# An empty piece between turning a tile and turning it back, in the last batch's first eight heads

## The chip, the cores and the metric

The kernel runs on one core of a Trainium2 chip. The metric is the device time of one execution in microseconds; the median of four runs stands for the kernel.

## The reference, cut to what matters

Two layers work on eight batches of 512 tokens of width 256. The first has a state-space mixer and a mixture of experts; the second has attention and another mixture of experts. The change lies in the second layer's attention, at its end:

```
scores = clip(q_h . k_h / 16) * decay(|i - j|)       # 16 heads of width 16, 512 x 512
attn   = softmax(scores)
out_h  = attn . v_h                                  # 512 x 16 for each head
y      = concat_heads(out_h) @ Wo                    # 256 x 256
x      = x + y + mixture_of_experts(xn)
```

Neither layer's other parts differ between the two kernels.

## The kernel before

The second layer is one hand-written order of instructions for all engines, made by Python generators while the kernel is built. The main loop runs over n = 0 to 130. The 128 steps are 8 batches x 4 groups of four heads x 4 tiles of 128 query rows; three more rounds of the loop drain what is left. The last batch (b = 7) has the steps 112 to 127.

In round n the loop issues, in this order:

1. The scores of step n: TensorE multiplies q and k for four heads (`s_ps`, line 1471), VectorE clamps each (line 1476), multiplies it by the decay band while taking its row maximum (line 1478), and negates the maxima (`ng`, line 1482). That is one block of nine instructions on VectorE, and ScalarE's exponentials of this step wait for its end.
2. The exponentials of step n - 1 on ScalarE (line 1486): heads 0 and 1, later 2, later 3.
3. In even rounds the values product of the two steps before (`o_ps`, line 1502).
4. The transposes of step n - 2, head by head: four 128x128 products into one of two banks (`p_ps`, line 1493), which ScalarE copies out (`pT`, line 1494). Heads 0 and 1 come first, then 2, then 3.

Between these stand slots, each a call of `fill()`. A call takes the first generator in a list of waiting work and runs it to its next `yield`; what is issued until then is one piece. The list `urgent` goes ahead of all else. An odd round has three slots: behind the scores, behind the transposes of heads 0 and 1, and at the end. An even round has four: behind the values, behind heads 0 and 1, between heads 2 and 3, and at the end. A generator that is at its end gives its slot to the next one. In the rounds up to 117 the slots hold the pieces of the experts; in 119 and 120 they hold the output projection of batch 6 (`finish`, line 1434).

For the batches 0 to 6 the division by the softmax's sum goes through memory (`divide`, line 1508). The last batch is divided on the chip. The values product of a group leaves 128 rows (four heads of 32 rows, of which 16 are output and one is the sum of the softmax) by 512 tokens, copied to `ol` (line 1515). When the second group is copied, in round 122, `first_heads` (line 1386) is put ahead in `urgent`. For each of the four tiles of 128 tokens it turns the two groups (`tq`, line 1392), so that tokens lie on the partitions; `columns` divides on VectorE (`smq`, line 1381, and `oq`, line 1383); and a second piece turns the result back (`tb`, line 1396), which ScalarE copies to `oT` (line 1397), the input of the output projection. `tq` and `tb` share one bank of PSUM (`bank`, one buffer), so that each waits for the reader of the one before. Here they are called tq0, tb0, ..., tq3, tb3.

Every engine works its instructions in the order in which they were issued. The class `Ending` (line 1400) does the same for the last eight heads, in the tail behind round 128, and `project` (line 1423) writes the last batch's output.

Of the kernel before, what the change touches and what calls it, by code (L numbers as in the profile page):

```python
# [59 lines left out]
def tile_kernel(ctx: ExitStack, tc: tile.TileContext, t, out: bass.AP):  # L60
# [292 lines left out]
    def bank(name, shape, tag="gen"):  # L353
        return mp.tile(shape, FP, name=name, tag=("e", "s")[tag] if isinstance(tag, int) else tag, bufs=2)
# [807 lines left out]
    with tc.tile_pool(name="a1", bufs=1) as p1, tc.tile_pool(name="a2", bufs=2) as p2, tc.tile_pool(  # L1162
# [214 lines left out]
        def columns(tq):  # L1377

            tq = tq.rearrange("p g (i r) -> p (g i) r", r=32)
            sm = p2.tile([P, 8], FP, name="smq", tag="smq")  # L1380
            V.reciprocal(sm, tq[:, :, AD])
            oq = p2.tile([P, 8, AD], FP, name="oq", tag="oq")
            V.tensor_tensor(oq, tq[:, :, :AD], bc(sm, 2, [P, 8, AD]), ALU.mult)
            return oq.rearrange("p h d -> p (h d)")

        def first_heads(oT, os):

            for c in range(TPB):
                at = slice(c * P, (c + 1) * P)
                tq = bank("tq", [P, 2, P])  # L1390
                for k in range(2):
                    T.transpose(tq[:, k, :], os[k][:, at], ident)
                oq = columns(tq)
                yield
                tp = bank("tb", [P, P])
                T.transpose(tp, oq, ident)
                A.copy(oT[:, 0, at], tp)
                yield
# [109 lines left out]
        def divide(b, g, op, od, rd, held):  # L1508


            if b == B - 1:
                if g == 0:
                    held.append(p1.tile([P, KC, S], FP, name="oT", tag="oT"))
                held.append(p1.tile([P, S], FP, name="ol", tag="ol", bufs=3))
                A.copy(held[-1], op)
                if g == 1:
                    urgent.insert(0, first_heads(held[0], held[1:]))
                return
# [258 lines left out]
```

## Time and profile before

| | |
|---|---|
| median of four runs | 2040.01 us (2034.94 to 2049.17) |
| the profiled execution | 2041.37 us, its span 2039.6 us |
| mean granted TensorE clock | 0.945 |
| busy: TensorE, VectorE, ScalarE, GpSimd | 89%, 70%, 58%, 31% of the span |
| last score product (step 127) | starts at 2010.86 us |
| last instruction of VectorE | starts at 2036.28 us |

Times in the profile are microseconds from the start of the span. PE is TensorE's products, PEld its weight loads, DVE VectorE, ACT ScalarE, POOL GpSimd. In a timeline a row is a run of like instructions: start, length, engine, line, operation, output and input, count, and in brackets how long the engine had been idle and what ended that. The steps are found by the score products (line 1471): the last group of eight records is step 127, and step 122 starts at 1972.74 us.

### The profile page before, as it was taken

The numbers are of one execution on the slowest core, as the hardware profiler recorded it, in microseconds if no ns is written. First come the engines' busy times: TensorE is split into PE (matmuls) and PEld (weight loads), VectorE is DVE, ScalarE is ACT, GpSimd is POOL, SyncE is SP. The second block draws the span as 40 slices with busy tenths as digits, with TensorE's granted clock in tenths as the row PEclk, the third lists the DMA queues.
The fourth block names the chain that finished last, engine by engine and source line by source line (L and its number), as shares of the span: only waits on it lengthen the run. The fifth ranks groups of instructions, "written<-read, shape, count | busy, mean of one in ns | idle before, by whom it ended". The sixth has DMA issues, their size and how long they took to land. (4 is left out here: it accounts for less than half of the span.)

```text
span 2039.6 us, 33308 instructions
## 1 busy us (share of the span) xinstructions
PE 1822.3 (89%) x11760; PEld 1229.8 (60%) x11760; DVE 1436.3 (70%) x3311; ACT 1177.7 (58%) x2536; POOL 628.8 (31%) x572
## 2 busy tenths in 40 slices
PE   5666899999999999988585999899999999999987
PEld 4333676766767777754353555566666666666654
DVE  4784766667576665758764898777777777777785
ACT  2243353545445354544532668677878777787875
POOL 0038644646455454643540025300000000000030
PEclk9877999999999999998786899999999999999998
DMA  7113565655456565634443345422231321313170
GB/s 268 62 42 103 203 212 171 213 164 192 154 168 205 178 206 176 203 87 128 146 138 99 124 133 198 144 84 85 49 103 38 98 69 51 88 51 100 34 166 11
DMA packets 150439, 262.34 MB, mean 129 GB/s; under 512 B 22361, under 2 KB 107212, under 8 KB 138368
## 3 DMA queue, kind: packets, MB, share of 16 engines
q1 hardware_dynamic: 112288, 139.62, 21.9%
q0 software_dynamic: 28512, 110.92, 17.7%
q10 hardware_dynamic: 9472, 9.67, 1.4%
q8 instruction: 93, 1.52, 0.3%
q14 instruction: 74, 0.61, 0.1%
HBM read 188.46 MB, written 76.68 MB: 130 GB/s over the span
## 5 line engine op out<-in xcount | busy, mean ns | idle before, releaser
L1476 DVE TENSOR_SCALAR s<-s_ps 128x512 f32<-128x512 f32 x512 | 317.8, 683 | 172.1 <-PE s_ps L1471 169.3
L1486 ACT ACTIVATE s<-s,ng 128x512 f32<-128x512 f32 x512 | 351.2, 728 | 14.0 <-DVE ng L1482 13.9
L1478 DVE CUSTOM_DVE_ANT_0 s<-s,band 128x512 f32<-128x512 f32 x512 | 322.9, 686 | 0.0
L1493 PE MATMUL p_ps<-ident,s 128*128 128x128 f32 x2048 | 289.1, 282 | 32.8 <-ACT pT L1494 32.8
L1494 ACT COPY pT<-p_ps 128x512 f32<-128x512 f32 x512 | 280.0, 590 | 43.3 <-PE p_ps L1493 36.3
L1493 PEld LDWEIGHTS p_ps<-ident,s 128*128 128x128 f32 x2048 | 240.2, 144 | 99.1 <-ACT pT L1494 59.2
L1281 POOL DMA_INDIRECT x<-e_yo,e_to x28 | 43.5, 1552 | 595.1 <-ACT e_yo L1280 539.4
L746 PE MATMUL pj<-xT,w_in 128*128 128x512 f32 x384 | 201.9, 652 | 17.0 <-DVE cv L759 14.9
L1471 PE MATMUL s_ps<-kT,qT 16*128 16x512 f32 x1024 | 161.8, 665 | 13.8 <-DVE s L1476 9.3
L559 PEld LDWEIGHTS h_ps<-xdT,w 128*128 128x128 f32 x1248 | 149.2, 193 | 22.3 <-issue 21.7
L559 PE MATMUL h_ps<-xdT,w 128*128 128x128 f32 x1248 | 152.9, 276 | 2.8 <-DMA w<-in_w_dram,w_idx 2.8
L759 DVE SCALAR_TENSOR_TENSOR cv<-pj,w_conv_w,cv 128x511 f32<-128x511 f32 (+2 forms) x192 | 143.0, 745 | 11.0 <-ACT cv L755 7.0
L577 PE MATMUL y_ps<-w,hT 128*128 128x256 f32 x624 | 147.3, 380 | 0.0
L922 POOL TENSOR_TENSOR au<-da,half 128x512 f32<-128x512 f32 x64 | 77.7, 1214 | 224.4 <-PE seg L938 121.1
L1502 PE MATMUL o_ps<-pT,vt 128*32 128x256 f32 x2048 | 136.3, 397 | 0.0
L577 PEld LDWEIGHTS y_ps<-w,hT 128*128 128x128 f32 x624 | 116.1, 191 | 31.6 <-issue 17.6
L746 PEld LDWEIGHTS pj<-xT,w_in 128*128 128x128 f32 x384 | 71.8, 205 | 100.1 <-issue 91.0
L996 POOL TENSOR_TENSOR yT<-yT,ex 128x512 f32<-128x512 f32 (+1 forms) x48 | 58.6, 1220 | 225.8 <-DVE ex L995 158.6
L1262 PE MATMUL e_hp<-e_xdT,e_w 128*128 128x256 f32 x448 | 122.3, 396 | 2.2 <-ACT e_xdT L1247 0.8
L1275 PE MATMUL e_yp<-e_w,e_hT 128*128 128x256 f32 x448 | 119.0, 388 | 0.1
L1502 PEld LDWEIGHTS o_ps<-pT,vt 128*32 128x32 f32 x2048 | 66.0, 113 | 87.5 <-issue 54.0
L951 ACT ACTIVATE mt<-seg,mid 64x64 f32<-64x64 f32 x512 | 109.5, 309 | 0.8
(296 smaller groups left out, 3016.7 us busy)
## 6 DMA issues: line engine op xcount, KB each, us to landing
ex<-exd SPq DMA_DIRECT2D x96, 128.0 KB
u<-in_u_dram SPq DMA_DIRECT2D x16, 512.0 KB
xtd<-xT SPq DMA_DIRECT2D x16, 512.0 KB
fr<-fdd SPq DMA_DIRECT2D x64, 128.0 KB
xT<-xtd SPq DMA_DIRECT2D x15, 512.0 KB
od<-os SPq DMA_DIRECT2D x28, 256.0 KB
e_w<-in_ei_dram SPq DMA_DIRECT2D x7, 1024.0 KB
e_w<-in_eo_dram SPq DMA_DIRECT2D x7, 1024.0 KB
```

The lines of the kernel that those rows point to most:

```text
L559: T.matmul(hp[:, i, :], w1[:, k * FF + f * P : k * FF + (f + 1) * P], xdT[:, k * P : (k + 1) * P], start=(k == 0), stop=(k == KC - 1),)
L577: T.matmul(yp, hT[f // 4][:, f % 4, :], w2[:, f * DM : (f + 1) * DM], start=(f == 0), stop=(f == FC - 1))
L746: T.matmul(pj, w_in[:, k, o * P : (o + 1) * P], self.xT[:, k, :], start=(k == 0), stop=(k == KC - 1))
L759: V.scalar_tensor_tensor(cv[:, s:], pj[:, : S - s], conv_w[:, q, 3 - s : 4 - s], cv[:, s:], ALU.mult, ALU.add)
L1262: T.matmul(hp, w1[:, k, f * P : (f + 1) * P], xdT[:, k, :], start=(k == 0), stop=(k == KC - 1))
L1471: T.matmul(sp[i], self.q[r, cols], self.k[r, :], start=True, stop=True)
L1476: V.tensor_scalar(self.p[i], sp[i], -CLAMP, CLAMP, ALU.max, ALU.min)
L1478: V.tensor_tensor_reduce(out=self.p[i], in0=self.p[i], in1=band[:, at : at + S], scale=1.0, scalar=-3.0e38, op0=ALU.mult, op1=ALU.max, acc ...
L1486: A.activation(self.p[i], self.p[i], AF.Exp, bias=self.ng[:, i : i + 1])
L1493: T.transpose(pp[:, k, :], self.p[i][:, k * P : (k + 1) * P], ident)
L1494: A.copy(pT[i][:, :, cc * P : (cc + 1) * P], pp)
L1502: T.matmul(op[32 * i : 32 * i + 32, half * 2 * P : (half + 1) * 2 * P], self.v[:, k, h * (AD + 1) : h * (AD + 1) + 32], pT[i][:, k, :], st ...
```

## The change

`first_heads` gets a second `yield` between `columns` and the turning back. At that `yield` nothing has been issued, so the call of `fill()` that runs it returns with its slot empty, and the turning back goes into the slot after.

```diff
@@ -1392,6 +1392,7 @@
                     T.transpose(tq[:, k, :], os[k][:, at], ident)
                 oq = columns(tq)
                 yield
+                yield
                 tp = bank("tb", [P, P])
                 T.transpose(tp, oq, ident)
                 A.copy(oT[:, 0, at], tp)
```

The generator has twelve pieces instead of eight, four of them empty: it takes the slots from round 122 to the first of round 125, where it took those from 122 to the first of round 124. Lines behind 1394 have a number higher by one in the changed kernel.

## The prediction

> **What bounds the kernel now.** I read the page first, then narrowed. Section 1 and the clock row of section 2:
>
> ```profile
> PE 1822.3 (89%) x11760; PEld 1229.8 (60%) x11760; DVE 1436.3 (70%) x3311; ACT 1177.7 (58%) x2536; POOL 628.8 (31%) x572
> ...
> PEclk9877999999999999998786899999999999999998
> ```
>
> TensorE is busy 89% of the span, but that is an average; the change touches only steps 122 to 125 of 128, whose score products start at 1972.74, 1982.45, 1992.85 and 2001.04 us. So next the timeline of VectorE over that stretch (start, length, engine, line, idle before and its releaser):
>
> ```profile
> 1974.56 2.48 DVE L1476 TENSOR_SCALAR s<-s_ps 128x512 f32<-128x512 f32 x4
> ...
> 1984.63 2.48 DVE L1476 TENSOR_SCALAR s<-s_ps 128x512 f32<-128x512 f32 x4 [2.70 <-PE s_ps L1471]
> ...
> 1995.03 2.48 DVE L1476 TENSOR_SCALAR s<-s_ps 128x512 f32<-128x512 f32 x4 [1.53 <-PE s_ps L1471]
> ...
> 2002.28 2.48 DVE L1476 TENSOR_SCALAR s<-s_ps 128x512 f32<-128x512 f32 x4 [2.12 <-PE s_ps L1471]
> ...
> 2007.32 2.48 DVE L1476 TENSOR_SCALAR s<-s_ps 128x512 f32<-128x512 f32 x4
> ...
> 2012.36 2.48 DVE L1476 TENSOR_SCALAR s<-s_ps 128x512 f32<-128x512 f32 x4
> ```
>
> These are the first clamps of steps 122 to 127. Steps 125 and 126 follow each other in 5.04 us with no idle time: VectorE alone paces a step without pieces. Steps 122, 123 and 124 take 10.07, 10.40 and 7.25 us, together 27.72. VectorE's own work there is three blocks of 5.04 and four `columns` of about 0.53 (reciprocal start to product end), 17.2 us. About 10.5 us are stalls, and TensorE's timeline shows whose:
>
> ```profile
> 1976.70 1.04 PE L1493 MATMUL p_ps<-ident,s 128*128 128x128 f32 x8
> 1980.26 0.30 PE L1396 MATMUL tb<-ident,oq 128*128 128x128 f32 x1 [2.52 <-DVE oq L1383]
> ...
> 1984.95 1.92 PE L1493 MATMUL p_ps<-ident,s 128*128 128x128 f32 x8
> 1990.34 0.45 PE L1396 MATMUL tb<-ident,oq 128*128 128x128 f32 x1 [3.48 <-DVE oq L1383]
> ```
>
> Turning back (`tb`) waits for `oq`, and `oq` stands on VectorE behind the whole block of that step. All that follows on TensorE, the next score products among it, waits too; then VectorE waits for those. And the same eight transposes that took 1.04 us take 1.92 after the first stall. The stretches of 5 us say why (PE, PEld, DVE, ACT, POOL busy, granted clock, DMA):
>
> ```profile
> 1975.00:1980.00 5.00, 2.20 (x26) 1.28 (x18) 4.93 (x15) 2.56 (x5) 1.51 (x2) 1.00 1.09 355
> 1980.00:1985.00 5.00, 4.63 (x23) 2.42 (x24) 0.99 (x4) 3.97 (x8) 0.00 (x0) 0.65 1.02 378
> 1985.00:1990.00 5.00, 1.86 (x9) 1.46 (x7) 4.93 (x15) 1.17 (x2) 0.00 (x0) 0.50 0.14 55
> ...
> 2020.00:2025.00 5.00, 3.21 (x17) 2.25 (x16) 0.91 (x4) 3.13 (x9) 0.00 (x0) 0.74 0.00 0
> 2025.00:2030.00 5.00, 5.00 (x40) 3.50 (x42) 0.00 (x0) 2.34 (x4) 0.00 (x0) 0.57 0.00 0
> ```
>
> Cut finer, the granted clock is half from 1981.5 to 1998.5 us (17.0 us) and again from 2022.4 to 2029.3 us (6.8 us, in the tail).
>
> **What moves.** No instruction is added. Of the eight pieces (tq0 to tb3) tq0 stays in step 122 behind the values. Places before and after: tb0, behind transposes 0 and 1 of step 122, then behind transpose 2; tq1, behind transpose 2, then behind 3; tb1, end of step 122, then behind transposes 0 and 1 of step 123; tq2, just behind the scores of 123, then the end of 123; tb2, behind transposes 0 and 1 of 123, then the same place in 124; tq3, end of 123, then behind transpose 2 of 124; tb3, behind the values of 124, then behind the scores of 125. Each `columns` goes with its tq, each copy to `oT` with its tb. SyncE's and GpSimd's orders are as before, so no DMA moves. The empty slots take none from other work: experts and batch 6's projection are issued by then, and GpSimd issues its last transfer at 1978.71.
>
> **Step 122.** VectorE's block and first `columns` do not move, so tb0 still starts at 1980.26. What changes is around it. Transpose 2 (four products, 0.44 us) now runs ahead, as soon as its bank is copied, at about 1978.0 (first copy 1977.40 plus 0.5); the idle stretch shrinks from 2.52 to some 1.8 us. On ScalarE the copy of tb0, which idled 2.13 us with exponential 2 and a transpose copy queued behind it, now stands behind both. After tb0: transpose 3 (0.44), tq1 at 1980.92 (as before: it needs the bank that the copy of tb0 frees), 0.36, and the scores of step 123 at 1981.3 instead of 1982.45. They need 1.2 us until VectorE's first clamp at full clock (2001.04 to 2002.28) and 2.2 at half (1992.85 to 1995.03).
>
> **Step 123.** tb1 now stands behind those scores and two transposes; its `oq` is ready at about 1982, so the 3.48 us wait goes. What is late next is VectorE itself (5.04 + 0.53 = 5.57) or, at half clock, TensorE. **Step 124.** tb2's `oq` comes with the end of block 123, while TensorE is still in scores and values of 124: no wait that shows. So the sum is in the first clamp of step 125, now 2002.28, by three bounds of the clock:
> - No drop: clamps at 1982.5, +5.57 = 1988.1, +5.57 = 1993.6. Gain 8.6 us. TensorE keeps up: 4.39 us for a step without values (2001.04 to 2005.43), 5.43 with (2005.43 to 2010.86), some 0.4 for the pieces.
> - Half clock for 6.8 us, as in the tail, from 1981.5 to 1988.3: step 123 clamps at 1983.5; its TensorE work is scores 2.09, transposes 3.84, tb 0.45, tq 0.64, 7.0 in sum, so the scores of 124 start at 1988.3, clamps 1989.5, then 5.57 or 5.43 + 0.4 + 1.2 for the scores of 125: 1995.3. Gain 7.0 us.
> - Half clock throughout, as before: scores of 124 at 1988.3, of 125 after 2.09 + 3.64 + 3.84 + 1.09 = 10.7, at 1999.0, clamps 2001.2. Gain 1.1 us.
>
> I take the middle: about 1.8 us of idle time in one stretch is nearer to 2.52, which lost the clock, than to the 1.39 of 1949.18, which did not, and the tail's 1.59 at 2022.49 lost it as well; but the second stall, which kept it low, is gone, and the tail is the nearest row of a drop with dense work behind it.
>
> The Trainium skill (TensorE: Matmul & The Clock Gate, "The HAM clock gate") states that the clock falls after about one idle window of 3.4 us and returns after about one busy one. By that a wait of 1.8 us would cost no clock and the sum would be the first bound; but here 2.52 us did, and the return took 6.8 and 17.0, so the rows decide.
>
> **Step 125 and the tail.** tb3 stands behind the scores of 125 and needs `oq` from the end of block 124. In an undisturbed step TensorE ends its scores about 1 us ahead of VectorE's block (2010.86 + 1.1 against 2012.3 and 0.5 for `columns`), so it waits 1 to 1.5 us, with the four transposes of 125 and the scores of 126 behind it. These need 4.4 us at most, VectorE's next block 5.04: covered at full clock. The tail runs as before, earlier. Its clock loss cost transposes 3.70 instead of 2.5 and values 2.93 instead of 1.94, with the turns about 2.7 us. Where its idle time falls against the clock's decision is not set by this change; I give it one in two: 1.4 us.
>
> **Sum.** 7.0 + 1.4 = 8.4 us off 2041.37 (span 2039.6 and 1.8 around it) gives 2033.0. The median of the four runs is 1.4 lower, so 2031.6, told as 2032.
>
> **Rivals.** *No drop at all*: 8.6 with the tail as it is, 11.3 with the tail at full clock, 2031.4 to 2028.7. For it: the idle stretch is a third shorter. Against: 1.59 us sufficed in the tail. *The clock stays low*: the empty slots only shift the wait, 1.1 us, 2039. For it: the scores alone, 2 us a step at half clock, did not raise it at 1985 or 1995. Against: no second long gap. *Slower*: tb3's new wait in step 125 (1 to 1.5 us) and that step's usual wait for copies (1.15 to 1.39) fall together, the clock goes to half there and stays. Then steps 125 to 127 take 5.9, 9.6 and 5.9 us of TensorE at half clock, and the tail about 25.6 (three rounds of products 16.2, turns and projections 5.7, last sum and write 3.7); from scores of 125 at 1999.0 that ends the span near 2046, 6 to 7 us later than now, about 2047. It decides from the point where the half clock lasts longer than today's 17.0 + 6.8 us in all.
>
> **How the numbers follow.** Forecast 0.42, no drop 0.33, low clock 0.17, slower 0.08. 0.5% is 10.2 us, about what a measurement of this kernel can tell from no change; the four runs span 14. Under 2029.8 come about 0.7 of the no-drop case and 0.45 of the forecast (tail at full clock is 9.7), in sum 0.43; over 2050 at most half of the slower case and bad luck, 0.05; 0.52 between. The range goes from 2028.7 less 4 for the scatter of a median to 2039 plus 2.
>
> **What would show it.** Right: the wait of tb on `oq` in step 122 near 1.8 us and none over 1.5 later; steps 122 to 124 in 19 to 21 us instead of 27.7; half clock for about 7 us instead of 17. Wrong: a wait over 2 us on tb3 with half clock behind it, or steps 123 and 124 still over 8 us.

## The result and the profile after

The changed kernel takes 2035.23 us in the median of 52 runs (2026.83 to 2048.31), beside 2041.41 us for the kernel before in 78 runs: a ratio of 0.9969, interval 0.9961 to 0.9978, or 6.3 us (4.5 to 8.0). The forecast was a gain of 8.4 us, 2032 on the scale of the four runs that were known; the time lies in its range, the gain told lies above the measured interval. The profiled execution took 2033.06 us (its span 2031.4), 8.3 us less than the 2041.37 of before's.

VectorE's timeline after, the rows that answer to those of before (start, length, engine, line, operation, idle before and releaser; lines behind the change count one more):

```profile
1973.56 2.48 DVE L1477 TENSOR_SCALAR s<-s_ps 128x512 f32<-128x512 f32 x4
...
1980.34 0.21 DVE L1381 RECIPROCAL smq<-tq 128x8 f32<-128x8 f32 x1 [1.22 <-PE tq L1392]
...
1982.35 2.48 DVE L1477 TENSOR_SCALAR s<-s_ps 128x512 f32<-128x512 f32 x4 [1.48 <-PE s_ps L1472]
...
1988.01 2.48 DVE L1477 TENSOR_SCALAR s<-s_ps 128x512 f32<-128x512 f32 x4
...
1993.79 2.48 DVE L1477 TENSOR_SCALAR s<-s_ps 128x512 f32<-128x512 f32 x4 [0.21 <-PE s_ps L1472]
...
2003.87 2.48 DVE L1477 TENSOR_SCALAR s<-s_ps 128x512 f32<-128x512 f32 x4
```

These are the first clamps of steps 122 to 125 and of 127, and the one reciprocal that waited. Steps 122, 123 and 124 take 8.79, 5.66 and 5.78 us instead of 10.07, 10.40 and 7.25: 20.2 instead of 27.7. The idle brackets show where: step 123's clamps waited 1.48 us for scores instead of 2.70, step 124's and 125's no more than 0.21 instead of 1.53 and 2.12. The `columns` of tq1 still waited 1.22 us for its turned tile; that of tq3 no longer waited. In the kernel before, their two rows were

```profile
1981.39 0.21 DVE L1381 RECIPROCAL smq<-tq 128x8 f32<-128x8 f32 x1 [1.27 <-PE tq L1392]
...
1992.96 0.21 DVE L1381 RECIPROCAL smq<-tq 128x8 f32<-128x8 f32 x1 [2.77 <-PE tq L1392]
```

In sum VectorE's idle time in these steps falls from 10.4 to 2.9 us. So 7.5 us of the 8.3 lie here; 1.0 us was there already when step 122 began (1973.56 against 1974.56) and is not the change's, and the tail gave 0.2 back. TensorE's timeline shows what became of the two long waits:

```profile
1977.04 0.66 PE L1494 MATMUL p_ps<-ident,s 128*128 128x128 f32 x4 [0.29 <-ACT pT L1495]
1979.18 0.33 PE L1397 MATMUL tb<-ident,oq 128*128 128x128 f32 x1 [1.48 <-DVE oq L1383]
...
1983.97 0.42 PE L1397 MATMUL tb<-ident,oq 128*128 128x128 f32 x1
1984.18 1.92 PE L1494 MATMUL p_ps<-ident,s 128*128 128x128 f32 x8
...
1989.71 1.09 PE L1494 MATMUL p_ps<-ident,s 128*128 128x128 f32 x8
1990.64 0.27 PE L1397 MATMUL tb<-ident,oq 128*128 128x128 f32 x1
```

One head's transposes now run ahead of tb0, whose wait shrinks from 2.52 to 1.48 us; the 3.48 us wait of step 123 is gone, since tb1 and tb2 find their `oq` ready. Eight transposes still take 1.92 us at 1984, but 1.09 again at 1989.7. The stretches of 5 us (busy times of the five engines, then the granted clock):

```profile
1975.00:1980.00 5.00, 2.69 (x20) 2.05 (x20) 4.05 (x13) 2.93 (x7) 0.75 (x1) 1.00 1.04 394
1980.00:1985.00 5.00, 5.00 (x23) 3.31 (x23) 3.15 (x7) 3.80 (x8) 0.00 (x0) 0.53 0.90 332
1985.00:1990.00 5.00, 5.00 (x51) 2.87 (x50) 4.83 (x15) 3.61 (x6) 0.00 (x0) 0.79 0.03 13
...
2010.00:2015.00 5.00, 2.70 (x21) 1.92 (x19) 0.57 (x3) 3.98 (x9) 0.00 (x0) 0.95 0.00 0
2015.00:2020.00 5.00, 5.00 (x24) 3.58 (x24) 0.34 (x2) 2.85 (x6) 0.00 (x0) 0.50 0.00 0
```

Cut finer, the clock is half from 1980.3 to 1987.1 (6.8 us instead of 17.1) and, in the tail, from 2014.5 to 2021.3 (6.8 us as before).

### The profile page after: what moved, and what is told of

Same layout as the page of the kernel before. It is cut to its first block, busy times and chain, and to the rows that moved or that the text cites. A ratio compares the mean times of both kernels' runs of the same rounds, so it can differ in the third digit from the quotient of the medians.

```text
span 2031.4 us, 33310 instructions
## 1 busy us (share of the span) xinstructions
PE 1819.9 (90%) x11760; PEld 1228.3 (60%) x11760; DVE 1435.9 (71%) x3311; ACT 1178.8 (58%) x2536; POOL 628.3 (31%) x572
```

## The experiments

The theory: the gain is two things, waits that end and clock that is kept, and each depends on whether a turning back stands ahead of the next scores while its `oq` is still behind the same step's block on VectorE. The main rivals: the clock is a side effect that VectorE hides; the distance between turning and turning back counts tile by tile; one tile is all.

Two places in each profile tell the theories apart better than the whole time does, whose runs of one kernel spread over 7 to 25 us: from the first clamp of step 122 to that of step 125, and from the first clamp of step 127 to the end of the span. Each row is one execution, the profiled one. In us:

| kernel | 122 to 125 | half clock there | 127 to end | half clock there | ratio to before |
|---|---|---|---|---|---|
| before | 27.7 | 17.1 | 27.3 | 6.8 | |
| changed | 20.2 | 6.8 | 27.5 | 6.8 | 0.9969 (0.9961 to 0.9978) |
| e1 before, kept busy | 22.9 | none | 26.7 | 3.4 | 0.9968 (0.9952 to 0.9984) |
| e3 a step later | 16.9 | none | 27.6 | 3.4 + 3.4 | 0.9945 (0.9921 to 0.9970) |
| e4 joined | 27.9 | 17.1 | 25.5 | none | 0.9994 (0.9979 to 1.0009) |
| e6 changed, tail kept busy | 20.2 | 6.8 | 25.9 | none | 0.9950 (0.9931 to 0.9969) |
| e2 changed, kept busy | 18.9 | none | 26.7 | 3.4 | 0.9993 (0.9974 to 1.0013) |
| e5 first tile only | 24.0 | 6.8 | 26.5 | 3.4 | 1.0008 (0.9987 to 1.0029) |
| e7 a step later, tail kept busy | 16.9 | none | 26.8 | 3.4 | 0.9960 (0.9935 to 0.9984) |
| e9 a step later, copies early | 16.7 | none | 23.7 | none | 0.9931 (0.9908 to 0.9955) |
| e8 two empty pieces | 18.5 | 3.4 | 26.7 | 3.4 | 0.9990 (0.9964 to 1.0016) |
| e10 before, copies early | 27.6 | 17.1 | 23.8 | none | 0.9986 (0.9970 to 1.0002) |
| e11 changed, again | 20.2 | 6.8 | 25.6 | none | 0.9990 (0.9971 to 1.0008) |
| e12 as e9, again | 16.7 | none | 24.9 | 3.4 | 0.9950 (0.9927 to 0.9973) |

e2, e5, e7 and e9, and then e8 and e10 to e12, ran beside a kernel before of 2072 us on other chips. The extra time lies far ahead of the change: in e5's profile the scores of step 8 start at 1170.6 us (1170.4 in before's) and those of step 32 at 1394.9 (1356.7); from there to step 120 it is 605.4 us in both. So their ratios carry that scatter, and the columns in microseconds are the firmer reading. In e3, e7, e8, e9 and e12 a `columns` moves on to step 125, which takes 5.47 us instead of 5.04; that 0.4 us stands in neither column.

**e1: the waits kept, the clock kept too.** A helper writes transposes that nothing reads to a bank for transposes:

```diff
+        def warm(k, tile):
+            if k:
+                pp = psum.tile([P, TPB, P], FP, name="wm", tag="p_ps", bufs=2)
+                for j in range(k):
+                    T.transpose(pp[:, j % TPB, :], tile, ident)
 ...
                 yield
+                warm((18, 0, 40, 0)[c], os[0][:, at])
                 tp = bank("tb", [P, P])
```

> The kernel before, with transposes that nothing reads put into its two long idle stretches of TensorE: 18 ahead of tb0 in step 122, 40 ahead of tb2 in step 123. Every wait on oq stays where it was; only the clock can change. Theory (the stalls cost mostly through the clock that they lose): no half clock in steps 122 to 125, first clamp of step 125 about 22.6 us after that of step 122 instead of 27.7, so about 5 us less than before. Rival (the waits alone cost, the clock is a side effect that VectorE hides): the three steps stay near 27.7 us and the time within 1 us of before.

Measured: 2036.6 us beside 2042.09, 5.5 less by the medians and about 6.5 by the ratio. TensorE's timeline of e1:

```profile
1980.76 2.19 PE L1390 MATMUL wm<-ident,ol 128*128 128x128 f32 x18 [0.29 <-ACT pT L1501]
1982.89 0.33 PE L1403 MATMUL tb<-ident,oq 128*128 128x128 f32 x1
...
1987.70 4.59 PE L1390 MATMUL wm<-ident,ol 128*128 128x128 f32 x40 [0.36 <-ACT pT L1501]
1992.12 0.27 PE L1403 MATMUL tb<-ident,oq 128*128 128x128 f32 x1
...
1993.42 1.14 PE L1478 MATMUL s_ps<-kT,qT 16*128 16x512 f32 x8
```

The turnings back come no sooner in their steps, yet the scores behind them run in 1.14 us instead of 2.09, and the three steps take 22.9 us, 22.6 expected. 58 useless transposes gain 4.8 us: the rival falls.

**e2: the changed kernel with its one stall filled.** `warm((10, 0, 0, 0)[c], os[0][:, at])` at the same place of the changed kernel.

> The changed kernel, with 10 transposes that nothing reads in the idle stretch ahead of tb0 in step 122, the one stall that is left. Theory (what the shorter stall still costs is the half clock behind it, 6.8 us in the changed kernel's profile): no half clock there, first clamp of step 125 about 19 us after that of step 122 instead of 20.2, so 1 to 1.5 us less than the changed kernel, 7 to 8 less than before. Rival (VectorE hides that half clock): within 0.5 us of the changed kernel.

Measured: the three steps take 18.9 us, 19 expected. The whole time misses: 2071.32 beside 2072.68, 1.4 us less than before instead of 7 to 8, and its interval reaches no further than 5.4. Which part of the run takes the gain back is open; the steps read here do not. With e1 this makes a square: 27.7 and 22.9 us without and with the clock before, 20.2 and 18.9 after the change. At full clock the change is worth 4.0 us of waits; the other 3.5 of its 7.5 us are clock that it keeps. e2 also shows the wait at tb3 that the prediction had named:

```profile
2021.64 0.30 PE L1404 MATMUL tb<-ident,oq 128*128 128x128 f32 x1 [1.44 <-DVE oq L1383]
```

**e4: the opposite.** The `yield` between turning and turning back is taken out, so that each tile is one piece and all four stand in step 122:

```diff
                 oq = columns(tq)
-                yield
                 tp = bank("tb", [P, P])
```

> The opposite of the change: no yield between columns and turning back, all four tiles in the four slots of step 122. Theory (what counts is a turning back that stands behind its own step's block, ahead of the next scores): one wait of about 3.4 us in step 122 with everything behind it, then three short ones of about 1 us each at half clock, none in steps 123 and 124; first clamp of step 125 some 25 to 30 us after that of step 122, the time within 3 us of before. Rival (distance between turning and turning back is what counts, tile by tile): four long waits, at least 5 us more than before.

Measured: 2041.13 us beside 2042.09, no difference that the interval shows. TensorE's timeline of e4:

```profile
1980.81 0.30 PE L1395 MATMUL tb<-ident,oq 128*128 128x128 f32 x1 [3.39 <-DVE oq L1383]
...
1983.06 0.45 PE L1395 MATMUL tb<-ident,oq 128*128 128x128 f32 x1 [0.72 <-DVE oq L1383]
...
1985.50 0.44 PE L1395 MATMUL tb<-ident,oq 128*128 128x128 f32 x1 [0.71 <-DVE oq L1383]
...
1987.94 0.45 PE L1395 MATMUL tb<-ident,oq 128*128 128x128 f32 x1 [0.72 <-DVE oq L1383]
```

One long wait for the block, then three that are only VectorE's two instructions and the way there and back. With no distance at all the three steps take 27.9 us, as with before's one slot. So the rival's four long waits do not come: only the first tile waits for a block. That one wait, with 17.1 us of half clock behind it, costs as much as before's two.

**e5: the empty piece for the first tile alone.**

```diff
-                yield
+                for _ in range(1 + (1, 0, 0, 0)[c]):
+                    yield
```

> The empty piece for the first of the four tiles only; the pieces behind it shift by one slot. tb0 and tb1 then stand as well as in the changed kernel, but tb2 comes at the end of step 123 ahead of the next scores, and tb3 in step 124 in the middle of the transposes, each behind its own step's block on VectorE. Theory (a tile's place against its own step's block decides, not how many pieces are empty): about 1.5 us of wait for tb0, 2 to 4 for tb2 and tb3; half clock for over 10 us; first clamp of step 125 about 26 us after that of step 122, the time 0 to 3 us less than before. Rival (the gain comes from tb0's step alone): most of the changed kernel's 6 us.

Measured: the whole time tells nothing (2074.42 beside 2072.68). TensorE's timeline of e5 from tb0 to tb3:

```profile
2018.38 0.33 PE L1397 MATMUL tb<-ident,oq 128*128 128x128 f32 x1 [1.48 <-DVE oq L1383]
...
2021.42 0.47 PE L1397 MATMUL tb<-ident,oq 128*128 128x128 f32 x1
...
2027.27 0.30 PE L1397 MATMUL tb<-ident,oq 128*128 128x128 f32 x1 [1.34 <-DVE oq L1383]
...
2034.45 0.30 PE L1397 MATMUL tb<-ident,oq 128*128 128x128 f32 x1 [2.70 <-DVE oq L1383]
```

tb0 and tb1 stand as in the changed kernel, tb2 and tb3 wait for their blocks, as expected by place (tb2 only 1.34 us). The clock stayed full through these two waits, 2.70 us among them. The price was set too high: 24.0 us instead of 26, with 6.8 us of half clock instead of over 10. Against the rival: half of the local gain is there (3.7 of 7.5 us), not most; the other half needs the pieces of the other tiles.

**e8: two empty pieces per tile.** A third `yield` ahead of the turning back.

> Two empty pieces per tile instead of one. tb0 now comes at the end of step 122, behind all its transposes, with the scores of step 123 right behind it; tq1 and tb1 go behind those, to steps 123 and 124, and so on until tb3 in step 126. Theory: a wait of about 1 us is left at tb0, too short to lose the clock in most phases; first clamp of step 125 about 17.5 us after that of step 122 (20.2 in the changed kernel); 2 to 3 us less than the changed kernel. Rival (more empty pieces push work toward the tail and cost there): no less than the changed kernel.

Measured: 18.5 us for the three steps, 17.5 expected, and 2068.34 us beside 2071.84, too close to the changed kernel's 2066.9 of the same group (e11) to tell; from the first clamp of step 122 to the end of the span e8 takes 55.7 us and e11 55.9, so the gain of 2 to 3 us over the changed kernel does not show. The wait at tb0 is what was expected, its effect was not:

```profile
2011.55 0.33 PE L1398 MATMUL tb<-ident,oq 128*128 128x128 f32 x1 [0.99 <-DVE oq L1383]
2011.81 1.62 PE L1473 MATMUL s_ps<-kT,qT 16*128 16x512 f32 x8
```

Even a wait of 0.99 us, with the short gaps ahead of it, ended in half clock here: the scores behind it take 1.62 us.

**e3: each tile turned back one step after it was turned.**

```diff
-                yield
+                for _ in range(1 + (4, 1, 2, 1)[c]):
+                    yield
```

> As the changed kernel, but with the pieces spread so that each tile is turned back one step after it was turned: tq0 in step 122, tb0 behind two transposes of step 123, tq1 at its end, tb1 in 124, tb2 in 125, tb3 in 126. Theory: no turning back waits for the block of its own step, so no long idle stretch, no loss of clock in these steps, each step at 5.57 us; first clamp of step 125 about 16.8 us after that of step 122; 10 us less than before, 3 to 4 less than the changed kernel. Rival (the empty piece's gain is all that the slots can give, since VectorE paces the steps anyway): within 1 us of the changed kernel, 6 less than before.

Measured: 2030.79 us beside 2042.09, 11.3 less by the medians. VectorE's timeline of e3, steps 122 to 126:

```profile
1977.01 2.48 DVE L1477 TENSOR_SCALAR s<-s_ps 128x512 f32<-128x512 f32 x4
...
1982.98 2.48 DVE L1477 TENSOR_SCALAR s<-s_ps 128x512 f32<-128x512 f32 x4 [0.40 <-PE s_ps L1472]
...
1988.46 2.47 DVE L1477 TENSOR_SCALAR s<-s_ps 128x512 f32<-128x512 f32 x4
...
1993.93 2.47 DVE L1477 TENSOR_SCALAR s<-s_ps 128x512 f32<-128x512 f32 x4
...
1999.40 2.47 DVE L1477 TENSOR_SCALAR s<-s_ps 128x512 f32<-128x512 f32 x4
```

16.9 us, 16.8 expected: no turning back waits, and but for 0.40 us VectorE alone paces the steps, its block and one `columns` each. Step 125 has a `columns` too (5.47 us); up to the first clamp of step 127 e3 gains 10.4 us, the changed kernel 7.5. The rival, that the changed kernel had taken all there was, falls.

**The tail.** e6 puts `warm(14, ...)` between the transposes of round 128 and the turning of the last tiles; e7 does that in e3; e9 takes the wait away instead, in e3, by having ScalarE copy the first two tiles' last values right behind their product; e10 does so in the kernel before; e11 and e12 are the changed kernel and e9 again.

```diff
                         tails += [Ending(s.b, c, s_op, s.scratch[2]) for c in (s.c - 1, s.c)]
+                        if n == N:
+                            for one in tails:
+                                one.out()
 ...
                 if n == N:
                     for one in tails:
-                        one.out()
-                    for one in tails:
                         one.divide()
```

> The changed kernel, with 14 transposes that nothing reads in the tail's idle stretch (between the transposes of round 128 and the turning of the last tiles, 1.59 us idle). Theory: the tail keeps its clock, its sixteen transposes take about 2.3 us instead of 3.7 and its values 1.9 instead of 3.2; 2.7 us less than the changed kernel in executions that lose the clock there, 1 to 2.7 in the median, so 7 to 9 less than before. Rival (ScalarE's copies pace the tail): within 0.5 us of the changed kernel.

> Both of the better parts: each tile turned back one step after it was turned, and 14 unread transposes in the tail's idle stretch. Theory: the gains add, since they lie in different stretches: 11 us less than before from the first and 2 to 4 from the second, 13 to 15 in all. Rival (the tail's clock was kept by luck of phase): no more than 11.

> Each tile turned back one step after it was turned, and instead of unread transposes the cause of the tail's idle stretch taken away: ScalarE copies the last values of the first two tiles right behind their product, ahead of the transposes' copies of that round, so that the turning of the last tiles does not wait for it (1.59 us). Theory (the wait and the clock it loses both go): 2 to 4 us less than without the second part, 13 to 15 less than before. Rival (the copies now delay the transposes' copies by their 0.45 us, and the idle time only moves there): no more than 11.

> The kernel before, with only the tail's part of the last kernel: ScalarE's two copies ahead of round 128's transposes' copies. Steps 122 to 125 as before, 27.7 us with 17 us of half clock. Theory (the two gains lie in different stretches and add): last score product to the end of the span about 25.7 us instead of 28.7; 2 to 4 us less than before. Rival (the tail's gain came with the steps' better clock): within 1 us of before.

> The changed kernel itself, beside the others in the same chip's runs, so that they can be compared with it and not with runs of another chip: 5 to 8 us less than before, first clamp of step 125 about 20 us after that of step 122, if the gain does not depend on the chip; if it came from this chip's phase alone, within 2 us of before.

> Each tile turned back a step later and ScalarE's copies early, once more, beside the changed kernel: first clamp of step 125 16.8 us after that of step 122, last score product to the end 25.7 us; 12 to 15 us less than before and 5 to 8 less than the changed kernel if the two parts add; 11 or less if they do not.

The first line is TensorE's timeline of the changed kernel, the second of e6, the third of e9, each at the turning of the last tiles:

```profile
2014.03 0.33 PE L1416 MATMUL tq<-ident,osq 128*128 128x128 f32 x1 [1.59 <-ACT osq L1411]
```

```profile
2009.67 1.75 PE L1390 MATMUL wm<-ident,ol 128*128 128x128 f32 x14 [0.44 <-ACT pT L1501]
```

```profile
2048.47 0.27 PE L1416 MATMUL tq<-ident,osq 128*128 128x128 f32 x1
```

Filled, the tail keeps its clock (25.9 us from the first clamp of step 127 to the end, 27.5 in the changed kernel's first profile), and e6 takes 2032.75 us beside 2042.09; without the wait the tail takes 23.7 (e9) and 23.8 (e10), and 24.9 in e12, which lost 3.4 us of clock. The same 1.59 us wait lost 6.8 us of clock in that first profile and none in e11's, whose tail took 25.6 unaided. So the loss is worth 1.9 us and comes or does not come in the same program. Step and tail gains add: e10 has the tail's alone (27.6 and 23.8 us), e9 both (16.7 and 23.7). In whole times e10 is 4.8 us below before by the medians, with an interval (0.9970 to 1.0002) that just reaches no change. In whole times e9 is 13.4 us below before and e12 12.7; e12 is 7.8 below the changed kernel of the same group. So e9's version is ahead of both kernels. e7's whole time, 4.0 us below before by the medians (8.3 by the ratio) instead of 13 to 15, misses its expectation, while its steps (16.9 us) are as expected; its profile lost 3.4 us of clock at 2043, behind a wait of 1.74 us for ScalarE's copy in round 128; the same wait (1.75 us) lost none in e9. The rest of that miss is open. So is e11's, 4.9 us by the medians and 0.999 by the ratio, whose interval (0.9971 to 1.0008) includes no change: its steps show the same 20.2 us.

## Why the prediction was right, point by point

- *Step 122.* Right in kind and nearly in size: transpose 2 ahead of tb0, a wait of 1.48 us where some 1.8 was told, the scores of step 123 earlier by 1.2 us within their step.
- *Step 123, the bound of the clock.* The middle case held: half clock for 6.8 us, in all three profiles of the changed kernel's steps (changed, e6, e11), and 20.2 us for the three steps where 20.7 was forecast. The upper bound was 19.1; e2 shows 18.9 for it. The lowest case (clock low throughout) did not show in a profile. But one of the two reasons for taking the middle case is false as it stands: 1.8 us is nearer to the 1.39 that kept the clock (0.4 away) than to the 2.52 that lost it (0.7). What was left was the tail's 1.59 us, a wait that e11 shows without a loss, and the length was taken over from the tail and not worked out. So the choice of the case was in part luck.
- *Step 124.* No wait at tb2: right.
- *Step 125.* The wait of 1 to 1.5 us at tb3 was not there in the changed kernel, since the scores of 125 came late enough to cover it; it was there, 1.44 us, in e2, where they came earlier. The slower rival needed it to lose the clock; e2 kept the clock and lost 0.2 us in step 126.
- *The tail: the term that was mis-sized.* 1.4 us were booked for a clock loss of 2.7 us at one in two. The loss is worth 1.9 us (27.5 against 25.6 in e11): the values were put at 1.94 us at full clock, but they take 2.66 there in e11 (3.24 in the changed kernel's first profile). And booking it for the changed kernel alone had no ground: before's runs can miss it as well. In the profiles it was lost in both, a gain of -0.2. Without this term the sum is 7.0, within the interval of 4.5 to 8.0. (In the chances, 0.7 of 0.33 and 0.45 of 0.42 make 0.42, not 0.43.)
- *The clock rule.* The Trainium skill (TensorE: Matmul & The Clock Gate, "The HAM clock gate") states a free-running window of about 3.4 us. All half-clock stretches read here are 3.4, 6.8 or 17.1 us, whole numbers of such windows, and the tail's loss that comes and goes agrees with a window that runs freely. That a whole idle window is needed does not agree: waits of 0.99 (e8), 1.48 and 1.59 us lost the clock. Nor does the length of a wait decide: e5 kept it through 2.70 us. Laid on the grid of these windows, the fourteen profiles show this from 1900 us on: a window at full clock with TensorE busy 40% of it or less was always followed by half clock (eleven times), one with over 63% never; in between there are both.
- *How long it stays low.* On the same grid ten windows at half clock were 97% busy or more with at least 40% of their time in scores (16 rows of weights): each was followed by another at half clock. Nineteen as busy with at most 32% in scores were each followed by full clock. In before, TensorE was busy all through 1991.72 to 1995.13, 2.09 us of it scores, and the clock stayed low; it was busy all through 1995.13 to 1998.55 without scores, and the clock came back. The two windows between before's first and last scores at half clock were emptied by the second wait (58% and 41% busy). That fits 17.1 us against 6.8; no run changed the scores alone, so the cause is not shown.

## What to carry to other kernels

A hand-placed piece that reads a slow engine's result should be checked against what that engine has queued in the same step, and moved behind the next step's start rather than by one slot: by the first clamp of step 127 the slot gained 7.5 us, the step 10.4. On TensorE a wait of 1 to 3 us costs its own time and, in some executions, half clock behind it; so look at the granted clock behind each such wait, and at what TensorE does there, since it stayed low for 3.4 to 17.1 us. To size the two apart, fill the wait with products that nothing reads.

## What the runs showed of the hardware

After before's stall the clock stayed low for 17.1 us although TensorE was busy for whole stretches of it (4.66 of 5 us from 1990 on), and e4 shows the same; behind the shorter stall it came back after 6.8 us. Unread transposes of a tile kept the clock full through 4.6 us of waiting (e1). The same program, with the same 1.59 us wait in the tail, lost the clock there in one execution and kept it in another. And the kernel before took 30 us longer on two other chips; in all profiles from there the stretch from step 8 to 32 takes 217 to 227 us, instead of 186 to 193 in the others.
